# A four-layer graph network on one core: two batches that keep their adjacency matrix on chip and open the last stage, second-pass buffers in batch order, warm-up matmuls without the identity

## The chip, the core and the metric

The kernel runs on one core of a Trainium2 chip. A core has five engines that run side by side, each with its own instruction order: TensorE (PE in the profile; its weight loads are shown apart as PEld), VectorE (DVE), ScalarE (ACT), GpSimd (POOL), and SyncE (SP), which here only issues transfers. Operands lie in SBUF, matmul results in PSUM (eight banks), inputs, outputs and parked intermediate results in DRAM. The metric is the time of one execution in microseconds (us), as the median of several runs.

## What is computed

There are 32 batches of 512 nodes with 128 features (x) and a symmetric 0/1 adjacency matrix of 512 x 512 with ones on its diagonal (adj, 1 MB per batch as f32). Four layers follow each other, each on `h = relu(layernorm(x))` and each adding its result to x:

```python
# layer 0: attention, masked by adj
v, q, k = relu(h @ Wv.T + bv), relu(h @ Wq.T + bq), relu(h @ Wk.T + bk)
x = x + softmax(where(adj, q @ k.T, -9e15)) @ v
# layer 1: A_norm = D^-1/2 (adj + I) D^-1/2
dyn = conv1d(h[:, -128:, :])            # on the last 128 nodes
lw = lstm(dyn)                          # 128 steps, all batches together
x = x + sigmoid((A_norm @ h) @ lw)
# layer 2: four graph layers, on h and its own earlier results
#   tanh([adj/|row| @ (n@ws+bs), n@wn+bn, adj.T/|col| @ (n@wd+bd)] @ wu + bu)
# layer 3
x = x + prelu(adj @ (h @ W.T) + bias)
```

The LSTM is the one place where the batches depend on nothing of each other but must run in step: 128 dependent steps, each for all 32 batches. Its input is layer 0's result for the last 128 nodes of every batch, and layer 1 of every batch needs its output.

## The kernel before

The kernel is written as three stages whose work a scheduler in the program mixes. It builds a list of operations with an estimated duration, their tiles, and a rank; it then places them one after another on the engines, always the one that can start first, and among those the one of lowest rank. The order that comes out is fixed when the kernel is built; on the chip every engine follows its own order and waits on semaphores.

- `pass_1(b)`, rank 10000 + 10 b: layer norm, keys, queries and values of batch b; these are stored in DRAM (`dkq`, `dv`). Attention for the last 128 rows only, which is what the LSTM needs.
- `lstm()`: 128 steps, ranks 0 to 127, ahead of everything else.
- `pass_2(b)`, rank 20000 + 10 b: attention for the other 384 rows. It is the filling between the LSTM's steps. For the batches in `EARLY` (0 to 19) it also does the sums `A @ h` of layer 1.
- `rest(b)`, rank 30000 + 10 b: the remainder of layer 1 and layers 2 and 3. Its first matmuls wait for the LSTM's end.

```python
    LATE = 2
    EARLY = range(20)
    FOLDS = (4, 7, 10, 13)
    MOVED = range(2, B - 2)
    ...
    BUFS = {"a": 2, "ar": 6, "x": 7, "xn": 5, "y": 5, "gs": 5, "inv": 4, "n0": 4, "n1": 4, "n2": 4, "n3": 4, ... "mm": 8, ...}
    ...
    plan = Plan(BUFS, ("ar", "x", "inv", "n0", "n1", "n2", "n3", "a"), "mm")
```

`BUFS` is the number of buffers of each tag; `mm` are the PSUM banks. The tags given to `Plan` are handed out strictly in the order in which the program text creates their tiles. `room` also keeps the last free buffer of `mm` and `gs` for work of the lowest rank that is not done yet (`by_rank[-1]`):

```python
            for t, n in need.items():
                spare = n + (t == self.banks and o.rank >= self.spared and self.left > 0)
                if len(slots[t]) < spare or len(slots[t]) == spare and t in self.kept and by_rank and o.rank > by_rank[-1].rank + 12:
                    return None
```

The head of the program makes an identity matrix for transposes, a bf16 copy of it, and a zero tile; 16 warm-up matmuls multiply the two. A PSUM bank that is to be filled with a bias before matmuls add to it gets such a zero matmul first, if nothing has marked it yet:

```python
    ident = const.tile([P, P], FP, name="f_ident")
    make_identity(nc, ident)
    ident_b = const.tile([P, P], BF, name="f_ident_b")
    nc.vector.tensor_copy(ident_b, ident)
    marks = const.tile([P, N], BF, name="f_marks")
    nc.vector.memset(marks, 0.0)
    ...
    def warm_up(rank, t, name, after=()):
        c = bank(name)
        PE(rank, t, lambda: nc.tensor.matmul(c.t, ident_b, marks, start=True, stop=True), [], [c], after=after)
    ...
        def mark():
            if not c.marked:
                nc.tensor.matmul(c.t, ident_b, marks[:, : c.size], start=True, stop=True)
```

The first pass loads x and, for the last 128 columns, the adjacency rows:

```python
        DMA(R, 256, lambda: nc.sync.dma_start(xc.t, x[b].rearrange("(t p) d -> p t d", p=P)), [], [xc])
        al = new("n1", (P, NT, P), f"f_al_{b}")
        DMA(R + 1, 256, lambda: nc.sync.dma_start(al.t, adj[b, :, NR:].rearrange("(t p) i -> p t i", p=P)), [], [al])
        xn = ln_full(R, xc, f"a{b}")
```

The second pass loads the whole matrix for an early batch and squares it on ACT (`squares`: the squares of 0 and 1 are the matrix itself, rounded for fast matmuls, and the row sums come with them); for the others it loads 384 of the 512 columns:

```python
    def pass_2(b):
        R = 20_000 + b * 10 if b < B - LATE else 30_000 + (b - B + LATE) * 10 + 15
        early = b in EARLY
        a = new("a" if early else "ar", (P, NT, N if early else NR), f"f_a_{b}")
        keys = new("inv", (P, N), f"f_k2_{b}")
        v = new("n3", (P, NT, P + 1), f"f_v2_{b}")
        xc = new("x", (P, NT if early else L, P), f"f_x2_{b}")
        ...
        if early:
            DMA(R, 1024, lambda: nc.sync.dma_start(a.t, adj[b].rearrange("(t p) j -> p t j", p=P)), [], [a])
            ar, deg = squares(R, b, a, "2")
        else:
            DMA(R, 768, lambda: nc.sync.dma_start(a.t, adj[b, :, :NR].rearrange("(t p) j -> p t j", p=P)), [], [a])
        ...                                        # 4 score matmuls, exp, mask, 12 sums
        DMA(R + 5, 192, lambda: nc.sync.dma_start(dx.t, xc.t[:, :L, :]), [(xc, t) for t in range(L)], [dx])
        ...                                        # layer norm statistics; sums_of_1 for early batches
```

The last stage loads matrix and x again, and checks on the side that the matrix is symmetric: its bf16 copy goes to DRAM (`das`), comes back transposed (`aT`), and DVE compares (`differ`). These three have rank R + 2, which the scheduler turns into 70 less than its stage's other work.

```python
    def rest(b, lw_after):
        R = 30_000 + b * 10
        a = new("a", (P, NT, N), f"f_a3_{b}")
        xc = new("x", (P, NT, P), f"f_x3_{b}")
        DMA(R, 1024, lambda: nc.sync.dma_start(a.t, adj[b].rearrange("(t p) j -> p t j", p=P)), [], [a])
        DMA(R, 192, lambda: nc.sync.dma_start(xc.t[:, :L, :], dx.t), [dx], [(xc, t) for t in range(L)])
        DMA(R, 64, lambda: nc.sync.dma_start(xc.t[:, L, :], dl.t), [dl], [(xc, L)])
        ar, deg = squares(R, b, a, "")
        ...
        if b in EARLY:                             # the sums of layer 1, from DRAM
            DMA(R, 256, lambda: nc.sync.dma_start(gT.t, kept_sums[b].t), [kept_sums[b]], [gT])
        else:                                      # or made here
            gT, first = sums_of_1(R, b, xc, ar, rs)
            diagonal(R, ar, OP.subtract)
        PE(R, T_TR, lambda: nc.tensor.transpose(plw.t, seq[:, :, b], ident), [], [plw], after=lw_after + ...)
        ...                                        # f_pl: gates; layer norm; f_xt: transpose
        POOL(R + 2, 1.4, lambda: nc.gpsimd.dma_start(das.t..., f32(ar.t)), [ar], [das], gap=6.0)
        plan.op({"SP": (3.0, lambda: nc.sync.dma_start_transpose(out=aT.t, in_=das.t))}, R + 2, [das], [aT], gap=4.0)
        ...                                        # differ: two compares on DVE, R + 2
        ...                                        # four layers: f_py projection, split into two parts (f_y),
        ...                                        #   f_pa aggregation with ar, scale, own weights, tanh (f_n)
        ...                                        # layer 3, store of out
```

The tiles are created in this order of batches, so the second-pass batches 30 and 31 stand between the first ones of the last stage:

```python
    for b in range(B):
        pass_2(b)
        if b in FOLDS:
            fold(FOLDS.index(b), 20_000 + b * 10)
        if b >= B - LATE:
            rest(b - B + LATE, end)
    for b in range(LATE, B):
        rest(b, end)
```

Of the kernel before, what the change touches and what calls it, by code (L numbers as in the profile page):

```python
# [13 lines left out]
P = 128  # L14
# [471 lines left out]
BF = mybir.dt.bfloat16  # L486
# [34 lines left out]
class Plan:  # L521
# [74 lines left out]
    def run(self, tc, queues):  # L596
        import bisect

        ops = self.ops
# [9 lines left out]
        for o in reversed(ops):  # L609
            behind[o] = max([0.0] + [behind[n] + self.HOP + n.gap for n in o.next]) + min(t for t, _ in o.engines.values())  # L610
        for o in ops:
            if o.rank >= self.last:
                k, sub = divmod(o.rank - self.last, 10)
                o.rank = self.last + 12 * k - 9 * max(0, k - 28) + 200.0 - (min(behind[o], 60) if sub == 5 else behind[o] + (70 if sub == 2 else 0.0))
        self.left = sum(o.rank < self.URGENT for o in ops)
# [9 lines left out]
        turn = {t: 0 for t in self.fifo}  # L625
# [54 lines left out]
        tiled = False  # L680
        by_rank = sorted((o for o in ops if o.rank >= 10_000), key=lambda o: -o.rank)
        while done < len(ops):
            best = None
            for e, cands in pools.items():
                first = None
                held = expected.get(e)
                for rank, no, o in cands:
# [16 lines left out]
                    if first is None or s < first[0] - 1e-9:  # L704
                        first = (s, o)
# [5 lines left out]
            s, e, o = best  # L711
# [38 lines left out]
def symmetric(ctx, tc, x, adj, weights, cols, rows, lstm_b, prelu_a, out, fail):  # L750
# [12 lines left out]
    nc = tc.nc  # L763
# [5 lines left out]
    MANY = 512 // (4 * B)  # L769
    LATE = 2  # L770
    EARLY = range(20)
# [30 lines left out]
    def new(tag, shape, name, dtype=FP):  # L802
        return plan.cell(sb, tag, shape, dtype, name)
# [22 lines left out]
    def PE(rank, t, fn, r=(), w=(), **k):  # L826
        return plan.op({"PE": (t, fn)}, rank, r, w, **k)
# [10 lines left out]
    def DMA(rank, kb, fn, r=(), w=(), **k):  # L838
        return plan.op({"SP": (max(0.45, t_dma(kb)), fn)}, rank, r, w, gap=2.0, **k)
# [21 lines left out]


    ident = const.tile([P, P], FP, name="f_ident")
    make_identity(nc, ident)
    ident_b = const.tile([P, P], BF, name="f_ident_b")
    nc.vector.tensor_copy(ident_b, ident)
    marks = const.tile([P, N], BF, name="f_marks")
    nc.vector.memset(marks, 0.0)
    ones = const.tile([P, P], FP, name="f_ones")
# [50 lines left out]
    def warm_up(rank, t, name, after=()):  # L920

        c = bank(name)
        PE(rank, t, lambda: nc.tensor.matmul(c.t, ident_b, marks, start=True, stop=True), [], [c], after=after)

# [6 lines left out]
    def fill(rank, dst, src, r, c, after):  # L931

        def mark():
            if not c.marked:
                nc.tensor.matmul(c.t, ident_b, marks[:, : c.size], start=True, stop=True)

        def act():
            mark()
            nc.scalar.copy(dst(), src)  # L939

        def dve():
            mark()
            nc.vector.tensor_copy(dst(), src)
        return plan.op({"ACT": (t_act(c.size), act), "DVE": (t_dve(c.size), dve)}, rank, r, [c], after)
# [158 lines left out]
    def pass_1(b):  # L1103
# [3 lines left out]
        al = new("n1", (P, NT, P), f"f_al_{b}")  # L1107
        DMA(R + 1, 256, lambda: nc.sync.dma_start(al.t, adj[b, :, NR:].rearrange("(t p) i -> p t i", p=P)), [], [al])
        xn = ln_full(R, xc, f"a{b}")

# [153 lines left out]
    def pass_2(b):  # L1264
        R = 20_000 + b * 10 if b < B - LATE else 30_000 + (b - B + LATE) * 10 + 15
        dkq, dv, dl, dx = kept[b]
        early = b in EARLY
        a = new("a" if early else "ar", (P, NT, N if early else NR), f"f_a_{b}")
        keys = new("inv", (P, N), f"f_k2_{b}")
        hT = new("xn", (P, NR), f"f_h2_{b}")  # L1270
        v = new("n3", (P, NT, P + 1), f"f_v2_{b}")
        xc = new("x", (P, NT if early else L, P), f"f_x2_{b}")
        DMA(R, 192, lambda: nc.sync.dma_start(hT.t, dkq.t[:, N:]), [dkq], [hT])
        DMA(R, 256, lambda: nc.sync.dma_start(keys.t, dkq.t[:, :N]), [dkq], [keys])
        if early:
            DMA(R, 1024, lambda: nc.sync.dma_start(a.t, adj[b].rearrange("(t p) j -> p t j", p=P)), [], [a])
            ar, deg = squares(R, b, a, "2")
            mask, rows_of = ar, lambda j: f32(ar.t[:, j, :NR])
        else:
            DMA(R, 768, lambda: nc.sync.dma_start(a.t, adj[b, :, :NR].rearrange("(t p) j -> p t j", p=P)), [], [a])  # L1280
            mask, rows_of = a, lambda j: a.t[:, j, :]
        DMA(R, 258, lambda: nc.sync.dma_start(v.t, dv.t), [dv], [v])
        DMA(R, 192, lambda: nc.sync.dma_start(xc.t[:, :L, :], x[b, :NR].rearrange("(t p) d -> p t d", p=P)), [],
            [(xc, t) for t in range(L)])
        if early:
            DMA(R, 64, lambda: nc.sync.dma_start(xc.t[:, L, :], dl.t), [dl], [(xc, L)])
# [24 lines left out]
        for t in range(L):  # L1311
            DVE(R, 0.26, lambda t=t: nc.vector.scalar_tensor_tensor(xc.t[:, t, :], po.t[:, t, :P], rinv[:, b, t : t + 1],
                                                                    xc.t[:, t, :], OP.mult, OP.add), [po, ri], [(xc, t)])
        DMA(R + 5, 192, lambda: nc.sync.dma_start(dx.t, xc.t[:, :L, :]), [(xc, t) for t in range(L)], [dx])
        mv = ln_stats(R, xc, range(L), f"r{b}")
# [16 lines left out]

    kept_sums = {}

    def squares(rank, b, a, name):

        ar = new("ar", (P, NT, N), f"f_ar{name}_{b}", FR)
        deg = new("dg", (P, NT), f"f_deg{name}_{b}")
        for t in range(NT):
            ACT(rank, 0.62, lambda t=t: nc.scalar.activation(ar.t[:, t, :], a.t[:, t, :], AF.Square,  # L1340
                                                             accum_out=deg.t[:, t : t + 1]), [a], [(ar, t), (deg, t)])
        return ar, deg
# [48 lines left out]

    def rest(b, lw_after):
        R = 30_000 + b * 10
        dkq, dv, dl, dx = kept[b]
        a = new("a", (P, NT, N), f"f_a3_{b}")
        xc = new("x", (P, NT, P), f"f_x3_{b}")
        DMA(R, 1024, lambda: nc.sync.dma_start(a.t, adj[b].rearrange("(t p) j -> p t j", p=P)), [], [a])
        DMA(R, 192, lambda: nc.sync.dma_start(xc.t[:, :L, :], dx.t), [dx], [(xc, t) for t in range(L)])
        DMA(R, 64, lambda: nc.sync.dma_start(xc.t[:, L, :], dl.t), [dl], [(xc, L)])
        ar, deg = squares(R, b, a, "")  # L1400
        dinv = new("dv", (P, TURN // NT, NT), f"f_dinv_{b}")
# [22 lines left out]
        plw = bank(f"f_plw_{b}", (P, P), whole=False)  # L1424
        PE(R, T_TR, lambda: nc.tensor.transpose(plw.t, seq[:, :, b], ident), [], [plw], after=lw_after + ([first] if first else []))
        lw = new("low", (P, P), f"f_lw_{b}")
# [8 lines left out]
        for t in range(NT):  # L1435
# [3 lines left out]
            [gT], [xc])  # L1439
        moved = b in MOVED  # L1440
        xn = ln_full(R, xc, f"c2{b}", moved)
# [56 lines left out]
        else:  # L1498
# [5 lines left out]
            end4 = PE(R, 4 * T_TR, back, [nodes[4]], [p4])  # L1504
        if b == B - 1:
            for k in range(2 * BUFS["mm"]):
                warm_up(R, 0.216, f"f_warm_{k}_{b}", [end4])
# [8 lines left out]
        agg3 = aggregate(R, hp, ar, p3a)  # L1516
        if b == B - 1:
            late.append(agg3)
# [50 lines left out]
    for b in range(B):  # L1569
        pass_2(b)  # L1570
        if b in FOLDS:
            fold(FOLDS.index(b), 20_000 + b * 10)
        if b >= B - LATE:
            rest(b - B + LATE, end)
    for b in range(LATE, B):
        rest(b, end)
    counted()
# [86 lines left out]
```

## Time and profile before

| | before |
|---|---|
| time, median of 3 runs | 1333.16 us (1332.34 to 1333.46) |
| profiled execution, first to last instruction | 1330.5 us |
| first matmul (warm-up) | 5.10 us |
| first matmul of the computation (transpose of batch 0) | 10.84 us |
| first and last matmul of the LSTM | 185.1 us, 505.6 us |
| mean granted TensorE clock | 0.996 |
| moved by transfers | 233.05 MB, 175 GB/s on average |

The profile counts an engine as busy while it executes instructions. For TensorE the ends of matmuls are modelled, so a busy TensorE is not one at its peak, and a hole in it is read more safely than its busy share. A wait that ends with a semaphore is put down to the instruction that released it last. A chain of dependent work can be followed in the timeline, where each row tells how long the engine had stood idle and what ended that.

The page's shares over the span in 40 equal slices (33 us each; tenths of busy time, and what the transfers moved) show that TensorE is nearly full all the time, that the transfers are heavy in the first half, and that the slice of 532 to 565 us is one of the few in which TensorE falls to 8:

```
PE   8999999999999998899999999999999999999996
DMA  7878888887576778855478659676266556573211
```

### The profile page before, as it was taken

How to read it: one execution, taken by the hardware profiler on the slowest of the kernel's cores; microseconds unless marked ns; L12 is line 12 of the kernel's file. 1: busy time of each engine (PE TensorE's matmuls, PEld its weight loads, DVE VectorE, ACT ScalarE, POOL GpSimd, SP SyncE). 2: the span in 40 equal slices, each digit the busy share in tenths (PEclk: the TensorE clock that was granted, in tenths of full speed). 3: DMA queues.
4: the chain of work that ended last, by engine and by line, in shares of the span. 5: the costliest groups of instructions: out<-in, count | busy, mean ns of one | idle time of the engine just before them, and what ended most of it. 6: DMA issues, size and time to landing. Idle time of an engine off the chain costs nothing. (4 is left out here: it accounts for less than half of the span.)

```text
span 1330.5 us, 26441 instructions
## 1 busy us (share of the span) xinstructions
PE 1289.0 (97%) x8833; PEld 989.8 (74%) x8833; DVE 1002.5 (75%) x3397; ACT 820.4 (62%) x2080; POOL 382.7 (29%) x729
## 2 busy tenths in 40 slices
PE   8999999999999998899999999999999999999996
PEld 6888877676666666677778777777877887777774
DVE  7899877887877778765686678677778787787644
ACT  5566668776856565755476556665666666675533
POOL 4655433222221135322133123232221232232101
PEclk9999999999999999999999999999999999999998
DMA  7878888887576778855478659676266556573211
GB/s 236 282 252 282 275 269 279 262 287 233 186 229 201 231 195 201 204 141 127 104 154 191 154 110 200 166 145 140 81 139 150 131 136 144 128 174 72 48 32 35
DMA packets 300449, 233.05 MB, mean 175 GB/s; under 512 B 138128, under 2 KB 247440, under 8 KB 300304
## 3 DMA queue, kind: packets, MB, share of 16 engines
q1 hardware_dynamic: 283408, 214.49, 56.7%
q0 software_dynamic: 16896, 16.78, 8.1%
q8 instruction: 72, 1.18, 0.4%
q14 instruction: 73, 0.60, 0.2%
HBM read 137.76 MB, written 62.00 MB: 150 GB/s over the span
## 5 line engine op out<-in xcount | busy, mean ns | idle before, releaser
L1387 PE MATMUL f_pa<-f_ar,f_y 128*128 128x512 f32 x1024 | 296.2, 426 | 4.4 <-DVE f_y L1370 4.0
L1387 PEld LDWEIGHTS f_pa<-f_ar,f_y 128*128 128x128 f32 x1024 | 189.3, 190 | 71.6 <-issue 30.9
L1478 PE MATMUL f_py<-f_wf,f_n 128*128 128x128 f32 x1280 | 173.8, 275 | 0.0
L1478 PEld LDWEIGHTS f_py<-f_wf,f_n 128*128 128x128 f32 x1280 | 164.5, 192 | 10.8 <-issue 3.6
L1493 ACT ACTIVATE f_n<-f_pa,f_bcol 128x512 f32<-128x512 f32 x128 | 88.0, 689 | 118.9 <-PE f_pa L1489 106.7
L1489 PE MATMUL f_pa<-f_n,f_wf 128*128 128x512 f32 x320 | 152.6, 592 | 0.0
L1340 ACT ACTIVATE f_ar<-f_a 128x512 fp32r<-128x512 f32 x208 | 129.1, 623 | 19.0 <-DMA f_a<-in_adj_dram 8.8
L1369 ACT CAST f_y<-f_py 128x512 fp32r<-128x512 f32 x128 | 74.7, 584 | 93.7 <-PE f_py L1478 82.8
L1485 DVE TENSOR_TENSOR f_pa<-f_pa,f_inv 128x512 f32<-128x512 f32 x128 | 87.5, 691 | 42.3 <-PE f_pa L1387 41.9
L1370 DVE TENSOR_TENSOR f_y<-f_py,f_y 128x512 fp32r<-128x512 f32 x128 | 87.2, 683 | 41.9 <-ACT f_y L1369 41.3
L1306 PEld LDWEIGHTS f_po<-f_v,f_e 128*128 128x128 f32 x768 | 98.8, 190 | 24.0 <-issue 9.7
L1306 PE MATMUL f_po<-f_v,f_e 128*128 128x129 f32 x768 | 111.2, 282 | 0.4 <-DVE f_e L1301 0.3
L1297 PE MATMUL f_s<-f_q,f_k 128*128 128x384 f32 x256 | 100.3, 500 | 0.6 <-ACT f_e L1300 0.4
L1446 POOL DMA_DIRECT2D f_das<-f_ar x32 | 29.7, 927 | 232.3 <-ACT f_ar L1340 107.4
L1489 PEld LDWEIGHTS f_pa<-f_n,f_wf 128*128 128x128 f32 x320 | 57.3, 190 | 43.8 <-issue 37.3
L1210 PE MATMUL f_z<-f_w,f_seq 128*32 128x128 f32 x2040 | 82.3, 278 | 6.2 <-DVE f_seq L1258 4.4
L1451 DVE SCALAR_TENSOR_TENSOR f_junk<-f_a,f_aT 128x1024 bf16<-128x1024 f32 x64 | 78.1, 1220 | 5.8 <-DMA f_aT<-f_das 4.5
L1210 PEld LDWEIGHTS f_z<-f_w,f_seq 128*32 128x32 f32 x2040 | 48.4, 109 | 43.8 <-ACT f_e L1300 10.0
L1478 PE MATMUL f_py<-f_wf,f_T_c 128*128 128x128 f32 x448 | 73.0, 276 | 2.8 <-ACT f_py L939 1.5
L1387 PE MATMUL f_pg<-f_ar,f_xp_c 128*128 128x512 f32 x256 | 75.0, 418 | 0.6 <-ACT f_xp_c L1377 0.6
L1387 PE MATMUL f_pg<-f_ar,f_xp_d 128*128 128x512 f32 x256 | 74.3, 415 | 0.4 <-ACT f_xp_d L1377 0.4
L1300 ACT ACTIVATE f_e<-f_s 128x384 f32<-128x384 f32 x128 | 61.5, 487 | 13.0 <-PE f_s L1297 11.2
(206 smaller groups left out, 2728.7 us busy)
## 6 DMA issues: line engine op xcount, KB each, us to landing
f_a<-in_adj_dram SPq DMA_DIRECT2D x52, 1024.0 KB
f_das<-f_ar POOLq DMA_DIRECT2D x32, 512.0 KB, 5.2
f_dkq<-f_kh SPq DMA_DIRECT2D x32, 448.0 KB
f_a<-in_adj_dram SPq DMA_DIRECT2D x12, 768.0 KB
f_dv<-f_v SPq DMA_DIRECT2D x32, 258.0 KB
f_v<-f_dv SPq DMA_DIRECT2D x32, 258.0 KB
f_x<-in_x_dram SPq DMA_DIRECT2D x32, 256.0 KB
f_al<-in_adj_dram SPq DMA_DIRECT2D x32, 256.0 KB
```

What stands on the lines that cost most here:

```text
L1210: nc.tensor.matmul(z.t[part, k, :, :], h, w[:, m : m + 4, part], start=False, stop=True, skip_group_check=True)
L1297: PE(R, t_mm(NR), lambda s=s, j=j: nc.tensor.matmul(s.t, keys.t[:, bass.ts(j, P)], q.t, start=True, stop=True), [keys, q], [s])
L1306: PE(R, t_mm(P), lambda t=t, j=j: nc.tensor.matmul(po.t[:, t, :], es[j].t[:, bass.ts(t, P)], v.t[:, j, :], start=(j == 0), stop=(j == NT - ...
L1340: ACT(rank, 0.62, lambda t=t: nc.scalar.activation(ar.t[:, t, :], a.t[:, t, :], AF.Square, accum_out=deg.t[:, t : t + 1]), [a], [(ar, t), ...
L1369: ACT(rank, t_act(N), lambda: nc.scalar.copy(parts.t[:, :, 0, :], src.t), [src], [(parts, 0)])
L1370: DVE(rank, t_dve(N), lambda: nc.vector.tensor_sub(parts.t[:, :, 1, :], src.t, f32(parts.t[:, :, 0, :])), [src, (parts, 0)], [(parts, 1)])
L1387: nc.tensor.matmul(pg.t, parts.t[:, j, k, :], ar.t[:, j, :], start=(k == 0 and j == 0), stop=(k == 1 and j == NT - 1))
L1451: nc.vector.scalar_tensor_tensor(junk, flat(a.t[:, 2 * k : 2 * k + 2, :]), 1.0, flat(aT.t[:, 2 * k : 2 * k + 2, :]), OP.mult, OP.not_equal ...
L1478: nc.tensor.matmul(py.t[:, j, :], nodes[n].t[:, bass.ts(j, P)], wf[:, W_F[i] + c, 0, :], start=False, stop=(c == nch - 1), skip_group_chec ...
L1485: before = DVE(R, t_dve(N), lambda pa=pa: nc.vector.tensor_mul(pa.t, pa.t, inv_row.t), [inv_row], [pa])
L1489: nc.tensor.matmul(pa.t, wf[:, W_F[i] + c, 1, :], nodes[n].t, start=False, stop=(c == nch - 1), skip_group_check=True)
L1493: ACT(R, 0.57, lambda pa=pa, n=n, i=i: nc.scalar.activation(n.t, pa.t, AF.Tanh, bias=bcol[:, i : i + 1]), [pa], [n])
```

## The change

Five things are changed together.

- Batches 26 and 27 (`FIRST`) are treated in the second pass like early ones as far as their data goes: they load the whole matrix into a buffer of tag `a`, square it, take the last 128 rows of x too, and keep all of it (`begun`). Their x is not stored. The last stage takes them first (`turn` 0 and 1), without loading anything of that again, then batches 0 to 25, then 28 to 31. Their sums of layer 1 are made in the last stage as before.
- `LATE` is 4: the second-pass batches 28 to 31 get ranks of the last stage's first turns, as filling for its opening. All tiles of the second pass are created before the first one of the last stage, so the tags that are handed out in order go to all second-pass batches first.
- The three operations of the symmetry check (`apart`) no longer count as undone work of low rank when the last PSUM bank and the last `gs` buffer are reserved.
- The warm-up and marking matmuls use the zero tile for both operands. The bf16 identity is gone, and the zero tile is made first.
- The adjacency rows of the first pass are asked for with the rank of the next batch, so that x of the next batch goes first.

```diff
+        apart = set()
         for o in ops:
             if o.rank >= self.last:
                 k, sub = divmod(o.rank - self.last, 10)
+                if sub == 2:
+                    apart.add(o)
...
-        by_rank = sorted((o for o in ops if o.rank >= 10_000), key=lambda o: -o.rank)
+        by_rank = sorted((o for o in ops if o.rank >= 10_000 and o not in apart), key=lambda o: -o.rank)
...
-    LATE = 2
+    LATE = 4
+    FIRST = [B - LATE - 2 + k for k in range(2)]
...
+    marks = const.tile([P, N], BF, name="f_marks")
+    nc.vector.memset(marks, 0.0)
     ident = const.tile([P, P], FP, name="f_ident")
     make_identity(nc, ident)
-    ident_b = const.tile([P, P], BF, name="f_ident_b")
-    nc.vector.tensor_copy(ident_b, ident)
-    marks = const.tile([P, N], BF, name="f_marks")
-    nc.vector.memset(marks, 0.0)
...
-        PE(rank, t, lambda: nc.tensor.matmul(c.t, ident_b, marks, start=True, stop=True), [], [c], after=after)
+        PE(rank, t, lambda: nc.tensor.matmul(c.t, marks[:, :P], marks, start=True, stop=True), [], [c], after=after)
...                                        # the same in mark()
-        DMA(R + 1, 256, lambda: nc.sync.dma_start(al.t, adj[b, :, NR:].rearrange("(t p) i -> p t i", p=P)), [], [al])
+        DMA(R + 11, 256, lambda: nc.sync.dma_start(al.t, adj[b, :, NR:].rearrange("(t p) i -> p t i", p=P)), [], [al])
...                                        # pass_2
-        a = new("a" if early else "ar", (P, NT, N if early else NR), f"f_a_{b}")
+        whole = early or b in FIRST
+        a = new("a" if whole else "ar", (P, NT, N if whole else NR), f"f_a_{b}")
...                                        # xc, loads and squares by "whole" too
-        DMA(R + 5, 192, lambda: nc.sync.dma_start(dx.t, xc.t[:, :L, :]), [(xc, t) for t in range(L)], [dx])
+        if whole and not early:
+            begun[b] = a, xc, ar, deg
+        else:
+            DMA(R + 5, 192, lambda: nc.sync.dma_start(dx.t, xc.t[:, :L, :]), [(xc, t) for t in range(L)], [dx])
...
-    def rest(b, lw_after):
-        R = 30_000 + b * 10
+    def rest(b, turn, lw_after):
+        R = 30_000 + turn * 10
+        if b in begun:
+            a, xc, ar, deg = begun[b]
+        else:
...                                        # the loads and squares as before
-        PE(R, T_TR, lambda: nc.tensor.transpose(plw.t, seq[:, :, b], ident), [], [plw], after=...)
+        PE(R, T_TR, lambda: nc.tensor.transpose(plw.t, seq[:, :, b], ident), [gT], [plw], after=...)
...                                        # "moved" and the two tests for the last batch go by turn
-        if b >= B - LATE:
-            rest(b - B + LATE, end)
-    for b in range(LATE, B):
-        rest(b, end)
+    for k, b in enumerate(FIRST + [b for b in range(B) if b not in FIRST]):
+        rest(b, k, end)
```

## The prediction

> **What bounds the kernel now.** I read the page's busy table first, then a table of busy time by stage, then the waits of TensorE over the whole span and inside the worst stage, and last the timeline of the first 20 us and of 505 to 552 us. The busy table:
>
> ```profile
> PE 1289.0 (97%) x8833; PEld 989.8 (74%) x8833; DVE 1002.5 (75%) x3397; ACT 820.4 (62%) x2080; POOL 382.7 (29%) x729
> ```
>
> TensorE (PE) is the bound, and only 1330.5 - 1289.0 = 41.5 us of it are idle. No TensorE work of weight is removed by the change, so what it can bring is idle time, and the stage table says where that lies (columns: stretch, its length, then busy us and instruction count of PE, PEld, DVE, ACT, POOL, granted clock, DMA share, GB/s):
>
> ```profile
> 0.00:5.00 5.00, 0.00 (x0) 0.00 (x0) 1.65 (x12) 1.49 (x2) 1.13 (x12) 1.00 0.39 110
> 5.00:10.00 5.00, 4.90 (x13) 1.76 (x14) 2.15 (x14) 0.49 (x1) 1.27 (x2) 1.00 1.01 284
> ...
> 20.00:40.00 20.00, 20.00 (x158) 17.99 (x157) 19.04 (x90) 13.56 (x27) 11.35 (x29) 1.00 0.85 281
> ...
> 185.00:508.00 323.00, 315.16 (x3255) 219.01 (x3256) 256.93 (x1167) 223.91 (x783) 80.02 (x151) 1.00 0.76 235
> 508.00:520.00 12.00, 11.56 (x75) 9.19 (x74) 9.62 (x33) 7.18 (x25) 7.39 (x12) 1.00 0.72 164
> 520.00:530.00 10.00, 7.75 (x58) 6.41 (x56) 7.29 (x33) 4.31 (x14) 5.08 (x8) 1.00 0.73 176
> 530.00:540.00 10.00, 6.97 (x36) 4.67 (x37) 7.47 (x24) 6.66 (x19) 4.80 (x8) 1.00 0.83 256
> 540.00:550.00 10.00, 7.12 (x31) 5.76 (x30) 5.17 (x17) 5.56 (x16) 3.23 (x4) 0.83 1.14 218
> ...
> 600.00:800.00 200.00, 196.95 (x1069) 153.18 (x1068) 137.53 (x351) 119.73 (x270) 49.22 (x81) 1.00 0.62 142
> 800.00:1200.00 400.00, 399.42 (x2148) 313.05 (x2147) 313.01 (x796) 258.66 (x564) 112.89 (x176) 1.00 0.63 144
> ```
>
> Three holes: the first 5.1 us (PE has nothing at all), the 42 us after the LSTM ends (its last matmuls start at 505.5; idle 0.44 + 2.25 + 3.03 + 2.88 = 8.6 us, and a clock of 0.83 at the end of it), and the last 10.5 us (a fixed tail: the last output store). The rest is spread thin: 7.8 us over the LSTM, 3.1 us from 600 to 800, 0.6 us from 800 to 1200. What ends the first two holes, from the waits of PE (us in total, times, longest):
>
> ```profile
> PE f_warm L923 <- DVE f_ident_b L866: 5.1, 1, 5.1
> ...
> PE f_pa L1387 <- DVE f_y L1370: 4.0, 2, 2.9
> ...
> PE f_pl L1432 <- DMA f_gT<-f_dgT: 1.8, 2, 1.1
> ```
>
> and from the timelines of PE and of ACT there (start, duration, what, and in brackets the idle time before it and what ended it):
>
> ```profile
> 544.39 5.54 PE L1387 MATMUL f_pa<-f_ar,f_y 128*128 128x512 f32 x16 [2.88 <-DVE f_y L1370]
> ...
> 541.81 0.63 ACT L1340 ACTIVATE f_ar<-f_a 128x512 fp32r<-128x512 f32 x1 [2.26 <-DMA f_ddi<-f_dT]
> ```
>
> The warm-up matmuls wait for the bf16 copy of the identity, which stands in DVE's order behind statistics of batch 0 that wait for its load. In the opening of the last stage the 2.88 us gap goes back to ACT: its copy of f_py (543.05) stands behind squares of a later batch's matrix that could not start before 541.81; that matrix was requested at 534.82, 7 us before, with the DMA engines full (share 1.14).
>
> **What the Trainium skill says.** "TensorE: Matmul & The Clock Gate", Part 1 (the HAM clock gate): TensorE begins at half clock, gets the full one after some 3.4 us of steady work, and falls back after an idle window. The trace agrees: the warm-up matmuls are 0.43 us apart from 5.1 to 9.8 us, then four weight loads come in 0.75 us; and after the gaps of 530 to 544 us 16 matmuls of 512 columns took 5.54 us where 4 take 1.07 us elsewhere (4.3 for 16): 1.2 us lost to the clock. The same page, "Architectural detail": ACT and DVE work strictly in order. That is the 541.81 line above, and it is what I have to look for in the new order. "Perfetto Trace Analysis", section Identifying the Most-Contended Engine: PE busy says little, the weight loads' busy time is a better measure. By it the hole is as large: 26.0 us of PEld in 508 to 550, where 800 to 1200 has 0.783 per us, that is 32.9 us for 42; the missing 6.8 us are 8.7 us of time.
>
> **The change part by part.**
>
> *Warm-up without identity.* Weights and moving operand are now both the zero tile; DVE sets it at 0.86 us (0.27 us), so the 16 warm-up matmuls start near 1.2 us instead of 5.1 and end near 1.2 + 5.9 = 7.1. But the first real transpose will not come 3.9 us earlier. In the new DVE order half of the statistics of batch 1 stand before the shift and normalization of batch 0, so batch 0 now waits for the load of batch 1. That load moves ahead of batch 0's adjacency rows (256 KB; the diff's R + 11): in the old trace it was used from 8.83 us; 256 KB at 284 GB/s are 0.9 us, so about 7.9. Then two statistics 0.45, shift 0.15, the third 0.25, three normalizations 0.85: transpose at about 9.6 against 10.84. Of the 6.5 us of idle before 20 us, the warm-ups give 3.9 back, 2.5 return between 7.1 and 9.6. I take 1.5 us. From 20 us on PE is full (20.00 of 20), so this passes on to the LSTM's start (185.1) and, as the LSTM is a chain of 128 steps of 2.5 us, to its end.
>
> *Two batches keep their matrix.* Batches 26 and 27 load 1024 instead of 768 KB in the second pass, square it there (4 x 0.62 us of ACT each, only moved), and skip the reload (1024 KB), the store of x (192) and its load (192): 2 x (1024 + 384 - 256) = 2.3 MB less of 233, with DMA at 0.6 to 0.8: nothing by itself. What counts is where. Old: batches 0 to 3 opened the last stage, each needing a matrix, x and its sums from DRAM, and the second-pass batch 31, meant as filling, could not run: it took its value buffer after one of the last stage, so its 12 matmuls came only after four layers of batch 0. All other filling was gone when the first transpose came (524.09). New order on PE after the LSTM's last matmul: scores of 29 and 30, sums of batch 27 (8 matmuls), batch 29, gates of 26, 0, 27, 1, the first transpose, then scores of 31, and batches 30 and 31 placed between the first layers of 26 and 27. So there are 16.4 us of filling (36 matmuls of 0.22, 9 of 0.65, a query projection 0.65, the 8 of batch 27 1.9), about as many as before, but 8.5 us of it lie behind the first transpose instead of 2.7. Worked with durations of the old trace: gates of 26 about 4 us after the last LSTM matmul; to its transpose the chain needs tanh 1.1, add 0.7, statistics 1.2, rsqrt 1.3 to 2, apply 0.9 and hops, about 8 us; filling between the two: 6.9 us. One us of idle. After that the chain projection, split (0.6 + 0.7), aggregation, scale, own weights has 1 to 3 us of filling at each step. I leave 2.5 us of idle in all: gain 8.6 - 2.5 = 6.1, plus 1.2 us of clock, as no gap near 3 us remains.
>
> *Fewer marks.* Filling a PSUM bank that no matmul had marked costs a 0.38 us matmul; four did that, none is left. Two fell into the hole. 0.5 us.
>
> *The matrix check leaves the reservation.* The check's transfers and compares rank 70 ahead, so the old rule that keeps the last PSUM bank for the oldest work held that bank back through most of the last stage. Now it is free to use. Where PE is full (800 to 1200) it brings nothing; in 600 to 800, idle 3.1 us, of which 1.5 ended at a bank fill on ACT, perhaps 0.5.
>
> The tail keeps its order (batches 28 to 31 last). Sum: 1.5 + 6.1 + 1.2 + 0.5 + 0.5 = 9.8 us, 0.7%.
>
> **Rivals.** (1) The wait moves to the two buffers of whole matrices: 26 and 27 hold both until their check is through, so batch 0's matrix is asked for late. For it: the check is a chain of store (5.2 us to landing), transposing load (about 5), compare 2.4, then the load, 5.7 to 7 us as seen at 527 and 534, and its squares stand on ACT before the first layer's tanh of 26; on SP it also stands behind batch 27's transposing load. My count: store issued about 4 us before the last LSTM matmul, compare at 12 to 14 after it, load asked for at 14.5, landed at 20.5, squares to 23, tanh of 26 due at 25. It fits by 2 us; if it does not, ACT stands, and 3 to 5 us come back: 1327 to 1328. (2) The head gives nothing, because the first stage is held by its transfers (share 0.82 to 0.89) and DVE (53.1 of 60 us) rather than PE: 1.5 less, 1325. If on the contrary batch 0 doesn't wait for batch 1, 3 us: 1322. (3) The opening was only shifting work and the idle returns in 550 to 800, where now turns 2 and 3 start late: 1330 to 1335. Against it: 30 turns with the same two buffers ran at 99.9% in 800 to 1200.
>
> **Range and chances.** 1333.2 - 9.8 = 1323.4, say 1323.5. Low end: all of the hole (9.8 with clock), 3 us of head, 2 us of the thin idle: 1317. High end: rival 1 with rival 2, or half of rival 3: 1331. 2% would be 1306.5, more than all idle time that is not the tail can give without luck; 2% slower has no mechanism in sight.
>
> **What would show it.** First warm-up near 1.2 us, first transpose at 9 to 10 (10.84); LSTM start near 183.6; PE idle in the 42 us after the LSTM 2 to 3 us with clock 1.00; no matmul of the marks; 800 to 1200 as before. Wrong if an ACT or DVE line there waits for f_a, f_aT or f_das for over 3 us, or if 550 to 800 holds more than 4 us of idle.

## The result, and the profile after

The changed kernel takes 1318.55 us in the median of four runs (1313.87 to 1319.71), against 1332.75 of the kernel before on the same chip: ratio 0.9894, with a 95% interval of 0.9861 to 0.9926. Two repeats beside other kernels gave 0.9872 (0.9847 to 0.9898) and 0.9881 (0.9850 to 0.9911). So it is faster by 14 to 17 us, 1.2%, which is less than 2%. Predicted were 9.8 us and 1323.5 us, with a range of 1317 to 1331.

The busy table of the changed kernel's page (busy us, share, instructions):

```profile
PE 1288.5 (98%) x8829; PEld 990.8 (75%) x8829; DVE 999.4 (76%) x3392; ACT 826.0 (63%) x2084; POOL 392.7 (30%) x729
```

Within this busy count TensorE's work is the same (1289.0 before) and what went is idle time: 1316.2 - 1288.5 = 27.7 us instead of 41.5. Four matmuls fewer are the four marks. The stage table of the changed kernel (stretch, length, busy us and instructions of PE, PEld, DVE, ACT, POOL, then granted clock, DMA share, GB/s):

```profile
0.00:20.00 20.00, 16.27 (x66) 10.38 (x67) 11.12 (x57) 7.76 (x14) 6.34 (x20) 0.83 0.71 209
20.00:185.00 165.00, 161.28 (x1204) 141.21 (x1203) 141.41 (x621) 106.69 (x211) 88.64 (x223) 1.00 0.84 267
185.00:505.00 320.00, 315.96 (x3258) 220.37 (x3258) 258.00 (x1178) 222.42 (x778) 82.36 (x155) 1.00 0.72 227
505.00:515.00 10.00, 10.00 (x69) 7.96 (x68) 8.92 (x35) 6.01 (x18) 2.71 (x5) 1.00 0.81 143
515.00:525.00 10.00, 8.41 (x51) 6.13 (x50) 7.54 (x26) 5.53 (x14) 2.99 (x4) 1.00 0.96 140
525.00:535.00 10.00, 8.66 (x57) 7.31 (x58) 9.85 (x32) 5.57 (x15) 2.00 (x3) 1.00 0.85 227
535.00:545.00 10.00, 10.00 (x62) 8.40 (x63) 6.30 (x26) 7.46 (x19) 6.61 (x14) 1.00 1.00 222
545.00:555.00 10.00, 8.95 (x49) 6.74 (x48) 8.32 (x20) 5.43 (x14) 3.75 (x7) 1.00 0.92 193
...
600.00:800.00 200.00, 199.12 (x1075) 154.59 (x1074) 142.05 (x369) 123.01 (x276) 51.47 (x80) 1.00 0.66 149
800.00:1200.00 400.00, 399.52 (x2141) 311.82 (x2140) 309.18 (x789) 257.49 (x570) 118.39 (x177) 1.00 0.65 145
```

The opening of the last stage, 505 to 555 us, holds 4.0 us of TensorE idle, and its clock stays at 1.00; the same five stretches of the kernel before add up to 8.6, with 0.83 in the last. The stage 600 to 800 went from 3.05 to 0.88, the LSTM's (185 to 505) from 7.8 to 4.0. The head went from 6.5 to 3.7 us of idle, but at a clock of 0.83. What is left in the opening, from TensorE's waits there (total us, times, longest):

```profile
PE f_py L1489 <- DVE f_hT_c L857: 1.7, 1, 1.7
PE f_py L1489 <- ACT f_py L941: 1.3, 1, 1.3
PE f_pa L1500 <- DVE f_pa L1496: 1.1, 1, 1.1
```

All three are steps within the first layers of the opening batches: the eviction of the transpose, a bank's fill with the bias, the scale. The waits for the split projection f_y (4.0 us in two) and for sums coming from DRAM (1.8) that stood there before are gone.

One distance sorts the runs better than the median alone: from the start of the LSTM's last matmul to the single small matmul near the end (f_pbad, the count of bad matrices). It is 803.3 us before (505.6 to 1308.9), and 788.7, 788.7 and 792.1 us in three profiles of the changed kernel, while the LSTM's end itself came at 506.1, 502.0 and 509.2 us in these three. So the LSTM's end scatters by 7 us between executions of one kernel, around the 505.6 of the one profile before, and the gain lies behind it. Of the 14.6 us there, idle time of TensorE from 506 to 1290 us is 7.1 (12.5 before, 5.4 after); the clock of 0.83 over 10 us is up to 1.7; and 3.5 us are work that the new order has already done by the LSTM's end. That is an estimate: I counted TensorE's instruction order with start-to-start distances seen in the traces (0.22 us for a matmul of 128 columns, 0.65 for 384, 0.23 for a fast one of 512): 785.3 us stand behind the last LSTM matmul before, 781.8 after; in all 1253.1 and 1252.7. These make 12.3. The rest is not settled. The aggregations `f_pa<-f_ar,f_y` are busy for 296.2 us before and 292.8 after, but part of that is the low clock, which is counted already.

### The profile page after: what moved, and what is told of

Its sections match the earlier page's. It is cut to its first block, busy times and chain, and to the rows that moved or that the text cites. A ratio compares the mean times of both kernels' runs of the same rounds, so it can differ in the third digit from the quotient of the medians.

```text
span 1316.2 us, 26405 instructions
## 1 busy us (share of the span) xinstructions
PE 1288.5 (98%) x8829; PEld 990.8 (75%) x8829; DVE 999.4 (76%) x3392; ACT 826.0 (63%) x2084; POOL 392.7 (30%) x729
## 5 line engine op out<-in xcount | busy, mean ns | idle before, releaser
L1395 PE MATMUL f_pa<-f_ar,f_y 128*128 128x512 f32 x1024 | 292.8, 422 | 0.7 <-ACT f_y L1377 0.7
L1395 PEld LDWEIGHTS f_pa<-f_ar,f_y 128*128 128x128 f32 x1024 | 188.2, 188 | 66.2 <-issue 28.0
L1348 ACT ACTIVATE f_ar<-f_a 128x512 fp32r<-128x512 f32 x208 | 129.1, 622 | 13.4 <-DMA f_a<-in_adj_dram 6.7
L1395 PE MATMUL f_pg<-f_ar,f_xp_d 128*128 128x512 f32 x256 | 77.9, 428 | 0.0
```

Of the source, the lines that this page charges most:

```text
L1395: nc.tensor.matmul(pg.t, parts.t[:, j, k, :], ar.t[:, j, :], start=(k == 0 and j == 0), stop=(k == 1 and j == NT - 1))
```

## The experiments

Each run was compared with the kernel before on the same chip, so the ratio counts; 0.001 is 1.3 us. The table has the LSTM's last matmul (E), the distance from it to f_pbad (D), TensorE's idle in 505 to 555 us (I), and the work counted behind the LSTM (W, an estimate as above), in us. E, D and I are each from one profile; two profiles of one instruction order differ in D by up to 3.4 us.

| kernel | ratio (95%) | E | D | I | W |
|---|---|---|---|---|---|
| before | 1 | 505.6 | 803.3 | 8.6 | 785.3 |
| changed | 0.9894, 0.9872, 0.9881 | 506.1, 502.0, 509.2 | 788.7, 788.7, 792.1 | 4.0, 3.8, 3.2 | 781.8 |
| changed, 24 warm-ups | 0.9867, 0.9874 | 504.5, 505.6 | 787.4, 789.1 | 3.3, 2.5 | 781.8 |
| changed, old head | 0.9941 (0.9920 to 0.9962) | 503.5 | 796.0 | 1.7 | 785.1 |
| changed, adjacency rows early | 0.9922 (0.9898 to 0.9945) | 506.0 | 795.0 | 1.3 | 785.1 |
| changed, check reserved | 0.9970 (0.9957 to 0.9983) | 504.9 | 801.7 | 9.6 | 781.8 |
| changed, none kept, 3 late | 0.9962 (0.9949 to 0.9975) | 505.9 | 796.8 | 6.8 | 781.5 |
| changed, none kept, 2 late | 0.9955 (0.9941 to 0.9969) | 507.8 | 799.2 | 9.8 | 781.5 |
| before, buffers in batch order | 1.0049 (1.0034 to 1.0064) | 508.7 | 810.8 | 6.2 | 784.3 |
| before, check unreserved | 0.9978 (0.9957 to 1.0000) | 509.8 | 803.4 | 8.8 | 785.2 |
| before, zero-tile warm-up | 0.9979 (0.9962 to 0.9995) | 501.3 | 805.9 | 9.2 | 785.3 |

**24 instead of 16 warm-up matmuls.** In the first profile of the change the clock fell behind the warm-up; eight more matmuls fill the gap.

```diff
-    for k in range(2 * BUFS["mm"]):
+    for k in range(3 * BUFS["mm"]):
         warm_up(HEAD, 0.43 if k < 8 else 0.216, f"f_warm_{k}")
```

> The changed kernel with 24 warm-up matmuls instead of 16, nothing else; the order of all other work is the same. Theory A: in the changed kernel the warm-ups end at 7.3 us, TensorE then stands idle until 9.2, the clock falls to 0.5 until about 17 us, and that is why the LSTM begins at 188.4 us instead of 185.1. Then eight more warm-ups (about 1.7 us) close the gap, the clock stays at 1.00 from 10 to 20 us, the LSTM begins near 185.5 to 186, and the time is 2 to 3 us below the changed kernel: 1316. Theory B: the first stage is held by its transfers, so the slow clock costs nothing: LSTM start 188, time 1318.5.

Measured: 1315.93 us (1312.5 to 1318.45), the clock at 1.00 through the head, the LSTM from 185.8 us. That was the expected time, and alone it reads as a confirmation; the repeats below take it back.

**The old head in the changed kernel.** The identity's bf16 copy and the old order of the tiles again, and the adjacency rows at the old rank.

```diff
+    ident_b = const.tile([P, P], BF, name="f_ident_b")
+    nc.vector.tensor_copy(ident_b, ident)
...
-        PE(rank, t, lambda: nc.tensor.matmul(c.t, marks[:, :P], marks, start=True, stop=True), [], [c], after=after)
+        PE(rank, t, lambda: nc.tensor.matmul(c.t, ident_b, marks, start=True, stop=True), [], [c], after=after)
...
-        DMA(R + 11, 256, lambda: nc.sync.dma_start(al.t, ...), [], [al])
+        DMA(R + 1, 256, lambda: nc.sync.dma_start(al.t, ...), [], [al])
```

> The changed kernel with the old head: warm-up with the bf16 identity, and the adjacency rows of the first pass asked for right after x of their own batch (R + 1). Theory A (the head as changed costs some 2.4 us, the opening of the last stage brings the whole gain): LSTM start 185.1, time 1315 to 1317, idle of TensorE in the 50 us after the LSTM about 4 us. Theory C (the earlier warm-up is part of the gain): 1320 to 1322.

Measured: 1325.57 us, slower than either theory had it. The head's two lines are worth some 7 us in the changed kernel, far more than the 1.5 predicted, and not through an earlier LSTM: it starts at 184.4 us here. D is 7 us longer, although the opening is even fuller (1.7 us idle). 3.3 us of the 7 are work left for later (785.1 for 781.8).

**Only the order of the buffers, in the kernel before.** All second-pass tiles are created before the first of the last stage.

```diff
     for b in range(B):
         pass_2(b)
         if b in FOLDS:
             fold(FOLDS.index(b), 20_000 + b * 10)
-        if b >= B - LATE:
-            rest(b - B + LATE, end)
-    for b in range(LATE, B):
+    for b in range(B):
         rest(b, end)
```

> The kernel before with one thing changed: all tiles of the second pass are created before those of the last stage, so that the buffers handed out in order go to second-pass batches first; no batch keeps its matrix, ranks, head and reservation as before. In the planned order 4.0 us of second-pass work on TensorE (before: 2.7; changed kernel: 8.5) lie behind the first transpose of the last stage. Theory D (buffer order is what opens the stage): 1322 or less, idle of TensorE in the 45 us after the LSTM 4 us. Theory E (the data kept on chip is what counts, as the first turns else wait for matrix, x and sums from DRAM): 1329 to 1333, idle there 6 to 9 us.

Measured: 1341.74 us (ratio 1.0049), slower than before and outside both theories. The order of the buffers lets the old filling run earlier (the last sums come 24.8 us of work after the LSTM instead of 51.3) and does not pay: the idle time of 600 to 800 us grows to 4.3 and that of 800 to 1200 to 6.2.

**No batch kept, three late ones.**

```diff
-    LATE = 4
-    FIRST = [B - LATE - 2 + k for k in range(2)]
+    LATE = 3
+    FIRST = []
```

> The changed kernel without kept batches: batches 26 and 27 load 384 columns and store x like the others, the last stage begins with batch 0; three second-pass batches (29 to 31) instead of four have ranks of the last stage. Head, buffer order and reservation as changed. 3.6 us of second-pass work lie behind the first transpose. Theory D: within 2 us of the changed kernel, 1317 to 1320.5. Theory E: 1325 to 1330, with TensorE waiting for squares of f_a or for f_gT from DRAM in the 45 us after the LSTM, 6 to 9 us idle there.

Measured: 1328.28 us, 10 us more than the change. The kept matrices matter, and Theory D falls. As this changes `LATE` too, a second run has two late batches, below.

**Adjacency rows early, zero-tile warm-up kept.** It splits the head's part: only R + 11 goes back to R + 1.

> The changed kernel with only the adjacency rows of each batch asked for where they were before (rank R + 1), the zero-tile warm-up kept. Theory R (what the head's part of the change brings comes from the later adjacency rows, because with them another order of the first pass is built, which leaves less TensorE work for the time after the LSTM): as slow as the run with the whole old head, about 1325.5 (ratio 0.994), with the LSTM starting near 184 and its idle time of 185 to 505 us near 6.5 rather than 4. Theory W (the zero-tile warm-up brings it): as the changed kernel, 1318.5 to 1320 (ratio 0.9894).

Measured: 1323.66 us, ratio 0.9922 beside 0.9872 of the change on the same chip. It stands near the old head's 0.9941, so most of it is the rank of the adjacency rows (Theory R, though its figure of 0.994 is at the edge of the interval), and 2 to 3 us are left for the warm-up (an estimate; the intervals of the two runs overlap). The stage table of this kernel (columns as above):

```profile
185.00:505.00 320.00, 311.57 (x3186) 216.65 (x3187) 251.99 (x1154) 222.64 (x780) 76.67 (x143) 0.99 0.70 223
...
555.00:600.00 45.00, 43.69 (x230) 33.29 (x231) 31.68 (x91) 31.87 (x72) 14.18 (x24) 1.00 0.88 214
600.00:800.00 200.00, 198.52 (x1075) 154.43 (x1074) 150.85 (x379) 123.46 (x264) 53.05 (x88) 1.00 0.68 154
800.00:1200.00 400.00, 397.22 (x2130) 309.28 (x2129) 309.07 (x783) 255.77 (x561) 110.39 (x169) 1.00 0.64 141
```

TensorE idles 8.4 us during the LSTM (4.0 in the change), has 3.3 us more work left behind it, fills the opening with that, and then idles 5.6 us from 555 to 1200. What a rank in the first pass decides is thus seen 300 us later.

**The check's operations back in the reservation.**

```diff
-        by_rank = sorted((o for o in ops if o.rank >= 10_000 and o not in apart), key=lambda o: -o.rank)
+        by_rank = sorted((o for o in ops if o.rank >= 10_000), key=lambda o: -o.rank)
```

> The changed kernel with the matrix check's operations back in the reservation of the last PSUM bank. Theory S (the reservation shapes the opening: by the instruction order the first transpose of the last stage then comes after 20.8 us of other work instead of 12.1, with 0.9 us of filling behind it instead of 8.5): the opening gets 3 to 5 us of its idle time back, 1322 to 1325 (ratio 0.992 to 0.994). Theory T (as predicted: it is worth 0.5 us, where TensorE is not full): 1319 (ratio 0.9897), idle in 505 to 555 us near 4 as in the changed kernel.

Measured: 1329.88 us, 13.6 us more than the change on the same chip: the whole gain but 4 us, and beyond what either theory gave it. The timeline of TensorE in this kernel (start, duration, what, in brackets the idle before it and its end):

```profile
519.73 0.81 PE L1300 MATMUL f_s<-f_q,f_k 128*128 128x384 f32 x2
522.49 1.56 PE L1300 MATMUL f_s<-f_q,f_k 128*128 128x384 f32 x2 [1.95 <-DVE f_lw L859]
...
528.20 0.61 PE L1309 MATMUL f_po<-f_v,f_e 128*128 128x129 f32 x4
533.25 2.52 PE L1309 MATMUL f_po<-f_v,f_e 128*128 128x129 f32 x10 [4.44 <-DVE f_e L1304]
535.56 0.95 PE L848 MATMUL f_xt_c<-f_ident,f_xn_c 128*128 128x128 f32 x4
```

and of the changed kernel:

```profile
517.59 0.81 PE L1300 MATMUL f_s<-f_q,f_k 128*128 128x384 f32 x2
518.24 0.60 PE L848 MATMUL f_xt_c<-f_ident,f_xn_c 128*128 128x128 f32 x4
...
521.10 2.30 PE L1300 MATMUL f_s<-f_q,f_k 128*128 128x384 f32 x6
525.06 1.16 PE L1489 MATMUL f_py<-f_wf,f_hT_c 128*128 128x128 f32 x8 [1.66 <-DVE f_hT_c L857]
526.06 0.81 PE L1300 MATMUL f_s<-f_q,f_k 128*128 128x384 f32 x2
```

With the check reserved, the chain to the first transpose runs late: ACT has the first gates of the last stage at 525.86 us (511.56 in the change), and DVE the normalized rows at 533.11 (516.61), so the transpose stands behind nearly all the second pass. The filling waits too. The 4.44 us are for the masked exponentials of a second-pass batch: ACT had the last of them done at 527.8 us, but in DVE's order the masking (L1304) stands behind two compares of the check and a step of the kept batch that waits for POOL:

```profile
532.56 0.16 DVE L1055 SCALAR_TENSOR_TENSOR f_sh_c<-f_mv_c,f_rs_c 128x4 f32<-128x4 f32 x1 [0.92 <-POOL f_rs_c L1036]
532.64 0.55 DVE L1304 TENSOR_TENSOR f_e<-f_e,f_a 128x384 f32<-128x384 f32 x1
533.11 1.16 DVE L1044 TENSOR_SCALAR f_xn_c<-f_x,f_mv_c,f_rs_c 128x128 f32<-128x128 f32 x4
```

The first layers, when they come, have little beside them. In the change, transpose, scores and projection alternate. Both carry the same work (W 781.8): the reserved kernel has 13.1 us of idle from 506 to 1290 us for 5.4, and clocks of 0.88, 0.84, 0.94 and 0.83 in the four stretches from 515 to 555, up to 5.1 us. That is 12.8 of the 13.0 us by which D differs.

**Only the zero-tile warm-up, in the kernel before.**

> The kernel before with only the warm-up's operands changed to the zero tile. Theory P (as predicted: the first stage is TensorE's, and an earlier warm-up without the later adjacency rows passes on): first real transpose near 10 us, LSTM start 0.5 to 1 us sooner than 185.1, time 1332 to 1333.5 (ratio 0.998 to 0.999). Theory Q (nothing reaches the LSTM, or a clock that falls in the gap behind the warm-up eats it): LSTM start 185 to 188, time 1333.5 to 1337 (ratio 1.000 to 1.002).

Measured: 1330.31 us, ratio 0.9979, at the end of Theory P's range: 2.8 us. In this profile the first transpose comes at 7.33 us and the LSTM starts at 182.2, both earlier than P said. TensorE's order is that of the kernel before, matmul for matmul, so no work has moved; D is 2.6 longer all the same, with 0.9 us more idle time from 506 to 1290 us (13.4 for 12.5) and clocks of 0.87, 0.84 and 0.95 in the opening (up to 3.4 us, for 1.7). Theory Q falls.

**The change again.** Nothing is edited.

> The changed kernel once more. If the fall of the clock behind the warm-up differs from execution to execution, this profile may show a clock of 1.00 at 10 to 17 us, and then the LSTM starts near 185.5 and the profiled time is 2 to 3 us lower than the other profile's; the median should again be 1317 to 1320 (ratio 0.988 to 0.991). If the fall belongs to the kernel, the LSTM starts near 188.4 again.

Measured: 1316.30 us. The clock fell again, later, and the LSTM nevertheless started at 184.0 us, earlier than in the first profile of 24 warm-ups with no fall. The two do not hang together as I had assumed; the eight profiles compared at the end of this section say more. The head of this profile, and after it that of the kernel with none kept and three late, which has the same 16 warm-ups:

```profile
9.37 0.75 PE L848 MATMUL f_xt_a<-f_ident,f_xn_a 128*128 128x128 f32 x4 [3.01 <-DVE f_xn_a L1044]
10.80 1.74 PE L1119 MATMUL f_pk<-f_kh,f_w 128*128 128x512 f32 x2 [0.69 <-ACT f_kh L853]
```

```profile
8.83 0.75 PE L848 MATMUL f_xt_a<-f_ident,f_xn_a 128*128 128x128 f32 x4 [2.01 <-DVE f_xn_a L1044]
10.27 1.12 PE L1119 MATMUL f_pk<-f_kh,f_w 128*128 128x512 f32 x2 [0.69 <-ACT f_kh L853]
```

The two projections of 512 columns take 1.74 us with the clock falling in them, and 1.12 at full clock.

**Only the check unreserved, in the kernel before.**

```diff
+                if sub == 2:
+                    apart.add(o)
...
-        by_rank = sorted((o for o in ops if o.rank >= 10_000), key=lambda o: -o.rank)
+        by_rank = sorted((o for o in ops if o.rank >= 10_000 and o not in apart), key=lambda o: -o.rank)
```

> The kernel before with only the matrix check's operations taken out of the reservation of the last PSUM bank. TensorE's instruction order in the opening of the last stage stays as before (first transpose after 16.9 us of other work, 2.7 us of filling behind it, 3 marks instead of 4). Theory S1 (the reservation matters only together with the kept matrices, because only then is there filling to place behind the first transpose): no gain, 1332.5 to 1335.5 (ratio 0.999 to 1.001), idle in 505 to 555 us near 8.6 as before. Theory S2 (the free bank alone is worth what the run with the check reserved lost, 10 to 13 us): 1320 to 1325 (ratio 0.990 to 0.993).

Measured: 1333.97 us, ratio 0.9978 (some 3 us), an interval from 6 us to nothing. D is 803.4 and the opening's idle 8.8, as before, in a profile of the slowest of the twelve executions. From 600 to 800 us its idle time is 1.4 us for 3.05: that is where the prediction had priced the bank. Theory S2 falls: alone the free bank is worth a few us at most, and 13 us in the change. The opening keeps the order of before, with 2.7 us of filling behind the first transpose; that only kept batches give the bank something to take is the reading of both runs together, not measured by itself.

**No batch kept, two late ones.**

> The changed kernel with no batch kept and two late second-pass batches, as before (the run without kept batches had three): head, buffers in order and unreserved bank stay. Theory E (the kept batches are what makes the opening start without loads, whatever the number of late batches): 1326 to 1330 (ratio 0.994 to 0.9975), idle in 505 to 555 us over 6. Theory F (three late batches were a bad choice and that was the loss): 1318 to 1322 (ratio 0.988 to 0.991).

Measured: 1328.34 us, as with three. Theory E holds. The timeline of ACT in this kernel shows why:

```profile
519.66 0.92 ACT L1303 ACTIVATE f_e<-f_s 128x384 f32<-128x384 f32 x2
527.39 0.63 ACT L1348 ACTIVATE f_ar<-f_a 128x512 fp32r<-128x512 f32 x1 [6.81 <-DMA f_a<-in_adj_dram]
...
529.24 0.47 ACT L1303 ACTIVATE f_e<-f_s 128x384 f32<-128x384 f32 x1
```

and TensorE's:

```profile
529.76 0.48 PE L1436 MATMUL f_plw<-f_ident,f_seq 128*128 128x128 f32 x1 [5.58 <-ACT f_e L1303]
```

ACT works in its order here. The squares of a matrix still in flight hold up an exponential whose scores were done at 522.8 us, and that holds up TensorE for 5.58 us. In the change the same wait of ACT for a matrix in the opening is:

```profile
ACT f_ar L1348 <- DMA f_a<-in_adj_dram: 2.3, 1, 2.3
```

The two other profiles of the change have 1.8 and 3.0 us. It is 9.6 us here, 8.0 with three late batches, and 4.7 (plus 2.3 put down to another load) in the kernel before from 506 to 556 us.

**24 warm-ups and the change, side by side.**

> The changed kernel with 24 instead of 16 warm-up matmuls, once more and in more rounds, beside the changed kernel itself. Theory G (the clock that falls behind the warm-up costs time in the end): 2 us less than the changed kernel of this same series, ratio 0.985 to 0.987, first two projections of 512 columns in 1.13 us. Theory H (the first stage has room, so the lost clock is taken back before the LSTM starts): within 0.7 us of the changed kernel, both 0.987 to 0.9885.

> The changed kernel beside the one with 24 warm-ups. First transpose near 9.3 us and, where the gap ahead of it is over 1.5 us, the first two projections of 512 columns in 1.7 to 2.1 us instead of 1.13. Theory G: 1318 to 1319.5 (ratio 0.988 to 0.9895). Theory H: 1316 to 1318 (ratio 0.987 to 0.9885).

Measured: 1319.12 and 1319.17 us, ratios 0.9874 and 0.9881: no difference, as Theory H had it. Its reason, that the lost clock is taken back, is not tested by this, for in this profile the clock fell even behind 24 warm-ups. Eight profiles share this order of the first pass (three of the change, two with 24 warm-ups, the one with the check reserved, two with none kept). In them the LSTM starts at 188.4 and 188.2 us where the clock was halved for 6.8 us in the head, at 184.0, 185.7 and 186.0 where it was for 3.4 us, and at 185.1, 185.8 and 186.9 where it was not. A long fall may thus cost the LSTM's start some 2 us; a short one shows nothing. The version that seemed to beat both kernels does not.

Not measured: kept batches with two late ones, one kept batch, and the later adjacency rows alone in the kernel before. So the number of late batches and the kept matrices are not separated in the presence of the kept ones.

## Why the prediction was right, and where it was not

The time lies in the range, and the change is within 2%; the gain is 4 to 7 us above the 9.8 of the sum. That it lies in the range is in part luck: the range allowed for gains from 2 to 16 us, and 3.5 us of moved work, which no term of the sum had, took the place of the earlier LSTM. (The three items of the range's low end add up to 14.8 us, which is 1318.4 and not 1317.) Point by point:

- **Opening, 8.6 to 2.5 us of idle, and 1.2 of clock: right, a little high.** Three profiles have 4.0, 3.8 and 3.2 us, a gain of 4.6 to 5.4 for 6.1; the clock stays at 1.00 in all. The mechanism is the predicted one: filling on both sides of the first transpose, and no loads ahead of it. The three runs that take away one of the two bring idle time back (6.8, 9.8 and 9.6 us), and two of them a low clock as well.
- **The reservation, 0.5 us: the step that failed as an attribution.** I read the new order off the built kernel, so its effect was in the opening's 6.1 us, but I put that down to the kept matrices alone and priced the bank only "in 600 to 800". Taken back, it costs 13 us; alone it brings some 3 us or nothing. The parts taken back one at a time (bank, kept matrices, head) lose 13.6, about 10 and 7 us, twice the gain. The first two are conditions of one effect, the opening, and not terms of a sum; the head's 7 us come another way, for without it the opening is even fuller (1.7 and 1.3 us idle).
- **The head, 1.5 us by an earlier LSTM: mis-sized, by a step that failed.** First warm-up at 1.19 us, first transpose at 9.19, 9.37 and 9.71, its wait for the second batch's load: as worked out. "From 20 us on PE is full, so this passes on to the LSTM's start" is wrong for this change: in three profiles the LSTM started at 188.4, 184.0 and 188.2 us, not at 183.6. The first pass has 3.7 us of TensorE idle between 20 and 185 us (3.5 before) and, by my count, 0.9 us more work in the new order, and the clock fell in the head. Without the later adjacency rows the step does hold: with the zero tile and the old rank the first transpose comes at 7.33 and 6.75 us and the LSTM starts at 182.2 and 183.6, against 184.4 to 186.0 in the four profiles with the old head. What the head's part is worth, some 7 us, I did not see coming: with the adjacency rows asked for later, another order of the whole first half is built, which gets 3.3 us more work done by the LSTM's end. I looked at R + 11 only for what it does to batch 0.
- **Marks, 0.5 us: none is left,** as predicted; no run measures the four by themselves.
- **Thin idle, 600 to 800, 0.5 us.** 3.05 became 0.88, 0.96 and 3.0 us in three profiles, so this is within the scatter.
- **Rival 1, the wait moves to the whole-matrix buffers: no.** In three profiles ACT waits 2.3, 1.8 and 3.04 us for f_a and DVE 2.4, 2.7 and 1.6 for f_aT, so the third just passes the 3 us that I had set as a sign of being wrong. **Rival 2** was right that nothing reaches the LSTM's start in the changed kernel; its reason, that TensorE does not hold the first stage, is not shown, and its 1325 did not come. **Rival 3: no,** but its sign appeared once: 550 to 800 us hold 2.0, 1.0 and 4.6 us of idle in the three profiles, against the 4 that I had set, with the gain still there in the third. Both limits lay inside the scatter of a single profile.

## What to carry to other kernels

When a scheduler makes the order, count how much work stands ahead of a long chain's end and how much behind it, for the whole program: a rank in the first pass moved 3.3 us across a chain that ended 300 us later. Parts of a change that all serve one stage should be priced as one, and taken back from the full version one by one, not only tried alone: here the lifted reservation brings some 3 us or nothing alone and 13 in company. And a version that is 2 us ahead in one series wants a second one beside its rival before it is believed.

## What was not expected of the hardware

- The granted clock falls after short gaps, in some executions and not in others. In the head it fell behind gaps of 3.01, 2.05, 1.86 and 1.59 us, each followed by one of 0.69; it did not with 2.01 and 1.64 and the same 0.69; and it fell behind 24 warm-ups with gaps of only 0.94 and 0.69:

```profile
8.96 0.75 PE L848 MATMUL f_xt_a<-f_ident,f_xn_a 128*128 128x128 f32 x4 [0.94 <-DVE f_xn_a L1044]
10.40 1.46 PE L1119 MATMUL f_pk<-f_kh,f_w 128*128 128x512 f32 x2 [0.69 <-ACT f_kh L853]
```

  The Trainium skill, "TensorE: Matmul & The Clock Gate", section "HAM oscillation — how this bites in real kernels", gives gaps of over some 3.4 us as the danger; here thin work between shorter gaps was enough. Its Part 1 says that the window runs freely, and the traces agree: in all 14 profiles the clock's records change only at multiples of 3.413 us from a start that differs by profile, so that the same gaps can fall into one window or two. Cut along this grid, the profiles have 5349 windows at full clock. The clock fell behind every one in which TensorE was busy for less than 44%, as the profile models it, and behind none with more than 53%; between these both occurred. The window of the fall behind 24 warm-ups, from 7.7 to 11.1 us, was 52% busy. In the prediction I counted on no loss where no gap nears 3 us.
- The LSTM's end moves between 502.0 and 509.2 us over three profiles of one kernel, while D moves by 3.4. Of these 7.2 us, 4.2 are there when the LSTM starts (184.0 and 188.2 us); its 128 steps took 317.7, 318.0 and 321.0 us, at a clock of 1.00 beside full transfers (DMA share 0.72). A single profile of this kernel tells little below 5 us.
